# Moving the second group normalization's dependent steps to the end of a stage, with fronts begun four stages later

## The chip, the core and the metric

The kernel runs on one core of a Trainium2 chip. The core has a matrix engine (PE; its weight loads are shown as PEld), a vector engine (DVE, VectorE), a scalar engine (ACT, ScalarE), POOL (GpSimd) and SP (SyncE), which here only issues DMA transfers, as POOL mostly does. Each engine takes its own instructions in the order in which the program gives them, and waits on semaphores for what other engines have to finish. Matrix products land in PSUM, which has eight banks; everything else sits in SBUF or in device memory.

The metric is the time of one execution on the device, in microseconds (us): the median over several runs.

## What is computed

Thirty-two images of 256 channels and 32 x 32 pixels pass through two layers, each after a group normalization over groups of 8 channels, each with a residual addition. The first is a 3x3 convolution on fp16 operands with its result clamped and rounded to fp16. The second is an involution: a small network makes 49 weights for each pixel and each of 16 channel groups, and every output pixel is the sum of its 7x7 neighbours, each times its weight.

```python
x = x + conv3x3_fp16(_gn(x), weight) + bias

z = _gn(x)
y = relu(bn(einsum('oc,bchw->bohw', w1, z)))         # 256 -> 64 channels
w = einsum('oc,bchw->bohw', w2, y) + b2              # 64 -> 16 groups * 49 taps
patches = all 49 shifts of pad(z, 3)
x = x + einsum('bgkhw,bgckhw->bgchw', w, patches)
```

`_gn` takes the mean and the variance over 8 channels and all 1024 pixels and returns (v - mean) / sqrt(var + eps).

## The kernel before

**The loop.** All of the kernel is one loop over steps `n` (line 556, stages in the words of the title), 16 steps to an image (`per`, line 547). What is given in a step is given to all engines in the order of the loop's body; nothing reorders it later. Below, the *phase* of a step is `n` modulo 16, and even and odd phases differ: image `b`'s products `sums` (line 508) come at even steps from n = 16b on, eight times two bands of columns and rows, and write one of two `acc` tiles; `add_windows` (line 530) adds the result into `x` on VectorE one step later, at odd phases. `weights` (line 403) comes at even phases, 18 steps ahead of the sums (`LEAD`): 32 small matmuls into two PSUM banks `pw0`, `pw1`, and four to eight VectorE additions (`evict`, line 424) that put the bias on and move them to the ring `w_sb`.

**From weights to sums.** SP writes the rows of `w_sb` to a buffer `wd` in device memory (`scatter`, line 465), and POOL and SP read it back in another layout into one of three `bands` (`load_bands`, line 478), nine steps ahead of the sums that use it. The image itself is read at line 106 by SP, 63 steps ahead (`LOAD`), and written at line 543.

**The front.** For each image a generator `front(b)` (line 284) gives what comes before the weights, one piece per step, from 56 steps ahead (`FRONT = -56`). So three or four fronts are alive at once, one image apart. Its steps t, counted from its begin, are:

| t | what | engine |
|---|---|---|
| 0, 1 | sums over the image, `add_up` (L214) | ScalarE |
| 2 | first group sum, `mean`, two squares with sums (L214) | VectorE, ScalarE |
| 5 to 7 | second group sum, `s`, `ve`; `r`; `finish` | both |
| 8, 9 | `xq`, the normalized fp16 image (L273) | ScalarE |
| 9 to 26 | convolution in four units of 2 x 9 matmuls (L332), each unit over four steps | PE |
| +3, +4, +5 of a unit | `q` (L346) empties `pc`, `x` (L348) adds bias and residual, `add_up` sums for the second normalization | VectorE, VectorE, ScalarE |
| 27 | first group sum, `mean`, squares of the second normalization | VectorE, ScalarE |
| 29, 30, 32 | second group sum, `s`, `ve`; `r`; `finish` | both |
| 33, 34 | `xn`, the normalized image (L273) | ScalarE |
| 36 | `py` (L377), then `y` (L388) | PE, ScalarE |
| 42, 44, 46, 48 | transposes `pt` (L396), copied to `pixels` (L400) | PE, ScalarE |

A group sum (`group`, line 218) is four VectorE instructions in a chain: `sums` (L222, in the second normalization's first group sum only), `across` (L224), `total` (L226), `back` (L230). `finish` is eight small ScalarE instructions in a chain.

**The order within a step.** In a step every live front is first advanced once, oldest first; this gives its piece. A front that yields `LATER` instead is advanced a second time, behind the first pieces of all fronts and still ahead of `sums`, `add_windows` and `weights`. Both normalizations give their two group sums in that second round.

**PSUM.** The eight banks are given out: `pw0` and `pw1` one each, `acc` two of two banks, `pc` one, and one that `py` and `pt` share. So a convolution unit's first matmul waits until `q` of the unit before has emptied `pc`; a unit's matmuls are at odd phases and `q` at phases 0, 4, 8 and 12.

The loop's advance of the fronts, before:

```python
later = list(fronts)
for part in range(2):
    for b in list(later):
        got = next(fronts[b], fronts)
        ...
        if got is not LATER:
            later.remove(b)
```

Of the kernel before, what the change touches and what calls it, by code (L numbers as in the profile page):

```python
# [69 lines left out]
SCRATCH = 4096  # L70
EARLY = CH + 4 + CH * CR
LATE = K1 * SW + 2 * 2 * SW
FRONT = -56
LOAD = -63
LEAD = 18

# [2 lines left out]
def tile_quant_conv_then_involution(  # L79
# [113 lines left out]
    def quantize_weights(kh):  # L193

        nc.vector.tensor_scalar(wq[:, kh], staged[kh], F16_MAX, -F16_MAX, ALU.min, ALU.max)  # L195
        nc.gpsimd.memset(bands[kh], 0.0)
        if kh == CH - 1:
            nc.gpsimd.memset(w_sb, 0.0)
# [74 lines left out]
                nc.scalar.activation(dst, src, AF.Identity, bias=self.off[:, one], scale=self.rstd[:, one])  # L273

    LATER = 1

    def backwards(at):

        step, n = at.ap[-1]
        return bass.AP(tensor=at.tensor, offset=at.offset + step * (n - 1), ap=[*at.ap[:-1], [-step, n]])  # L280
# [3 lines left out]
    def front(b):  # L284


        xt = x_tiles[b]

        def stages(n):
            for _ in range(n):  # L290
                yield

        gn = GroupNorm(b, 0)
        gn.begin(1)
        for h in range(CH):
            gn.add_up(xt, 0, h, 0, N, AF.Identity)
            yield
        yield LATER
        gn.means()
        gn.squares(xt)  # L300
        yield from stages(3)
        yield LATER
        gn.variances()
        yield
        gn.scales()
        yield
        gn.finish()

        for h in range(CH):
            yield  # L310
            gn.apply(h, [(xq[:, h], xt[:, h].rearrange("p (r c) -> p r c", c=W))])
        gn = GroupNorm(b, 1)
        gn.begin(N // NT)
        units = [(nt, mh) for nt in range(N // NT) for mh in range(CH)]
        for s in range(4 * len(units) + 2):
            u, i = divmod(s, 4)
            if u < len(units):
                nt, mh = units[u]
                if i == 0 and b == 0 and u % 2:

                    pc = ps_m.tile([P, NT], F32, tag="m", name="pc")
                elif i == 0:
                    pc = ps_c.tile([P, NT], F32, tag="pc", name="pc")
                for n in range(sum(CONV[:i]), sum(CONV[: i + 1])):


                    k = n if n < K0 * K0 else CH * K0 * K0 - 1 - n
                    kh, k = n // (K0 * K0), (k + K0 * K0 // 2) % (K0 * K0)
                    di, dj = k // K0 - PAD0, k % K0 - PAD0
                    r0, r1 = max(nt * RT, -di), min((nt + 1) * RT, H - di)  # L330
                    c0, c1 = max(0, -dj), min(W, W - dj)
                    nc.tensor.matmul(  # L332
                        pc.rearrange("p (r c) -> p r c", c=W)[:, r0 - nt * RT : r1 - nt * RT, c0:c1],
                        wq[:, kh, k, mh * P : (mh + 1) * P],
                        xq[:, kh, r0 + di : r1 + di, c0 + dj : c1 + dj],
                        start=n == 0,
                        stop=n == CH * K0 * K0 - 1,
                    )

            u, i = divmod(s - 3, 4)  # L340
            if 0 <= u < len(units) and i < 3:
                nt, mh = units[u]
                cols = slice(nt * NT, (nt + 1) * NT)
                if i == 0:
                    q = work.tile([P, NT], F16, tag="q", name="q", bufs=1)
                    nc.vector.tensor_scalar(q, pc, F16_MAX, -F16_MAX, ALU.min, ALU.max)  # L346
                elif i == 1:
                    nc.vector.scalar_tensor_tensor(  # L348
                        xt[:, mh, cols], q, bias_sb[:, mh : mh + 1], xt[:, mh, cols], ALU.add, ALU.add
                    )  # L350
                else:
                    gn.add_up(xt, nt, mh, nt * NT, (nt + 1) * NT, AF.Identity)
            yield
        yield LATER
        gn.means()
        gn.squares(xt)
        yield from stages(2)
        yield LATER
        gn.variances()
        yield  # L360
        gn.scales()
        yield from stages(2)
        gn.finish()
        xn = work.tile([P, CH, N], F32, tag="xn", name=f"xn_{b}", bufs=1)

        for h in range(CH):
            yield
            to = xn[:, h].rearrange("p (k d r j) -> p d k r j", d=SIDES, r=TR, j=JC)
            at = xt[:, h].rearrange("p (k r d j) -> p d k r j", d=SIDES, r=TR, j=JC)
            gn.apply(h, [(to[:, 0], at[:, 0]), (to[:, 1], backwards(at[:, 1]))])  # L370
        yield from stages(2)

        py = ps_m.tile([P, NT], F32, tag="m", name="py")
        for kh in range(CH):
            px = xn[:, kh].rearrange("p (a i n) -> p a i n", i=2, n=2 * JC)
            for i in range(2):
                nc.tensor.matmul(  # L377
                    py[i * CR : (i + 1) * CR],
                    w1_sb[:, kh, :],
                    px[:, :, i],  # L380
                    start=kh == 0,
                    stop=kh == CH - 1,
                )
        to = y_sb[b % 2].rearrange("p (k r d j) -> p d k r j", k=K, d=SIDES, j=JC)
        of = py.rearrange("p (k d r j) -> p d k r j", k=K, d=SIDES, j=JC)
        for d in range(SIDES):
            at = of[:, d]
            nc.scalar.activation(to[:, d], backwards(at) if d else at, AF.Relu, bias=bn_shift, scale=bn_scale)  # L388
        yield from stages(5)

        for m in range(0, M, 2):
            yield
            pt = ps_m.tile([P, 2, C], F32, tag="m", name="pt")
            for i in range(2):
                for h in range(CH):
                    nc.tensor.transpose(  # L396
                        pt[:, i, h * P : (h + 1) * P], xn[:, h, (m + i) * P : (m + i + 1) * P], ident
                    )
            to = pixels[(b * M + m) // 2 % NPIX].rearrange("p i a (v c) -> p (i a) v c", c=GC)
            nc.scalar.copy(to[:, :, ::2], pt.rearrange("p i (a v c) -> p (i a) v c", v=2, c=GC))  # L400
            yield
# [138 lines left out]
    def store(b, k):  # L540

        cols = slice(k * NT, (k + 1) * NT)
        nc.sync.dma_start(out[b].rearrange("(h p) n -> p h n", p=P)[:, :, cols], x_tiles[b][:, :, cols])
# [5 lines left out]
    def due(n, lag):  # L549

        b, i = divmod(n - lag, per)
        return (b, i) if 0 <= b < B else (None, None)

    with tc.manual_schedule():
        fronts = {}
        for n in range(FRONT, B * per + 2):
            b, i = due(n, FRONT)
            if i == 0:
                fronts[b] = front(b)
            later = list(fronts)  # L560
            for part in range(2):
                for b in list(later):
                    got = next(fronts[b], fronts)
                    if got is fronts:
                        fronts.pop(b)
                    if got is not LATER:
                        later.remove(b)
            if n in (FRONT + CH, FRONT + CH + 4):
                quantize_weights((n - FRONT - CH) // 4)
            b, i = due(n, 0)  # L570
            if b is not None and i % 2 == 0:
                sums(b, i // 2)
            b, i = due(n, 1)
            if b is not None and i % 2 == 0:
                add_windows(b, i // 2)
                if i // 2 == M - 1:
                    store(b, 1)
                    x_tiles.pop(b)

            b, i = due(n, 2)  # L580
            if b is not None and i == 2 * (M - 1 - SIDES):
                store(b, 0)
            b, i = due(n, -LEAD)
            if b is not None and i % 2 == 0:
                weights(b, i // 2 * WR)

            for part in range(2):
                b, i = due(n, -LEAD + 1 + part)
                if b is not None and i % 2 == 0:
                    for k in range(K):  # L590
                        if i // 2 == min((k + 1) * TR // WR, H // WR - 1):
                            scatter(b, k, part)
            b, i = due(n, LOAD)
            if i == 0 and b > 1:
                x_tiles[b] = load_x(b)

            b, i = due(n, 3 - 4 * NBAND)
            if b is not None and i % 4 == 0:
                load_bands(b, i // 4)
# [38 lines left out]
```

## Time and profile before

| | |
|---|---|
| median of 3 runs | 1353.61 us (1353.46 to 1360.37) |
| the profiled execution | 1351.29 us, its span 1349.5 us |
| PE busy | 1247.6 us, 92% of the span |
| POOL busy (issuing DMA) | 1012.5 us, 75% |
| VectorE busy | 827.1 us, 61% |
| ScalarE busy | 734.2 us, 54% |
| DMA | 361.85 MB, 268 GB/s over the span |
| PE waiting for bands, whole span | 44.2 us in 19 waits |

The profile is of one execution. Its page gives the busy time of each engine and of 16 DMA engines together, and the span in 40 slices of 33.7 us, in each of which a digit is the busy share in tenths. Other views list who waited for whom, single instructions in order of time with the wait ahead of each in brackets (length and releaser), and busy times in any stretch that one asks for. A wait "<- issue" is one for which the profile shows no releaser.

The chain of work that ended last gives PE 58% and DMA 24% of the span. The first of image 0's `x<-acc` additions starts at 93.4 us: what lies ahead of it is called the ramp below. The convolutions end three images before the kernel does, and what follows is called the tail.

### The profile page before, as it was taken

What the parts mean: (1) busy time and instruction counts of PE and PEld (TensorE: products, weight loads), DVE (VectorE), ACT (ScalarE), POOL (GpSimd) and SP (SyncE); (2) the same over time, 40 slices, a digit from 0 to 9 for tenths busy, and PEclk for the clock granted to TensorE, in tenths of its full rate; (3) what the DMA queues carried; (4) which work ended last, traced back from release to release, by engine and by line L of the source; (5) the groups of instructions that cost most, each with busy time, mean ns of one, the idle gap of its engine ahead of it and who ended that gap; (6) DMA issues with size and microseconds to landing.
All of it is one profiled execution on the core that took longest, in us unless ns stands there. A gap on an engine that the chain in (4) does not pass through costs nothing.

```text
span 1349.5 us, 65799 instructions
## 1 busy us (share of the span) xinstructions
PE 1247.6 (92%) x27648; PEld 757.6 (56%) x27648; DVE 827.1 (61%) x2539; ACT 734.2 (54%) x1731; POOL 1012.5 (75%) x1818
## 2 busy tenths in 40 slices
PE   4899999999989999999999999999999999999664
PEld 2355556655545665555566556555655556555453
DVE  5456656666656666666666566666666566566542
ACT  5875655555646556565555556555656565563300
POOL 9067777787778778877778777777877877788885
PEclk9999999999999999999999999999999999999997
DMA  6089999999999999999999999999999999999995
GB/s 227 6 236 295 270 271 284 283 278 296 282 271 286 297 287 281 298 282 281 267 285 287 260 282 282 271 284 284 288 285 278 274 280 278 277 285 262 282 270 157
DMA packets 360724, 361.85 MB, mean 268 GB/s; under 512 B 75056, under 2 KB 304752, under 8 KB 359152
## 3 DMA queue, kind: packets, MB, share of 16 engines
q1 hardware_dynamic: 278512, 229.38, 56.5%
q0 software_dynamic: 81920, 128.28, 33.5%
q8 instruction: 220, 3.60, 1.1%
q14 instruction: 72, 0.59, 0.1%
HBM read 176.60 MB, written 180.76 MB: 265 GB/s over the span
## 4 chain that ended last, share of the span: by engine, by line
PE 58%; DMA 24%; POOL 8%; issue 4%; DVE 3%; ACT 2%; SPq 1%; POOLq 0%; DVEq 0%; ACTq 0%
PE pc L332 24%; DMA band<-wd 19%; PE acc L522 18%; PE pw L411 10%; POOL band L497 8%; DMA wd<-w_sb 4%; PE py L377 3%; PE pt L396 3%; ACT junk L214 1%; DVE w_sb L435 1%; SPq L476 1%; DVE wq L195 1%; DVE x L538 1%; DMA band<-in_w 1%; DMA out<-x 0%
## 5 line engine op out<-in xcount | busy, mean ns | idle before, releaser
L497 POOL DMA_DIRECT2D band<-wd x1792 | 980.8, 550 | 320.5 <-DMA band<-wd 189.9
L435 DVE TENSOR_TENSOR w_sb<-pw,late_sb 128x224 f32<-128x224 f32 (+7 forms) x1280 | 331.4, 324 | 423.6 <-PE pw L411 423.4
L332 PE MATMUL pc<-xq,wq 128*128 128x496 f16 (+3 forms) x2304 | 535.1, 378 | 25.0 <-ACT xq L273 20.6
L522 PE MATMUL acc<-band,pixels 64*32 64x190 f32 (+1 forms) x16384 | 423.5, 330 | 55.5 <-DMA band<-wd 44.2
L522 PEld LDWEIGHTS acc<-band,pixels 64*32 64x32 f32 x16384 | 301.6, 107 | 164.7 <-issue 88.9
L332 PEld LDWEIGHTS <-wq 128*128 128x128 f16 x2304 | 206.3, 98 | 322.9 <-issue 106.7
L411 PE MATMUL pw<-late_sb,y 64*32 64x224 f32 (+1 forms) x8192 | 285.0, 330 | 14.1 <-issue 12.7
L538 DVE TENSOR_TENSOR x<-acc,x 128x380 f32<-128x380 f32 (+1 forms) x512 | 262.4, 513 | 35.5 <-PE acc L522 26.6
L411 PEld LDWEIGHTS pw<-late_sb,y 64*32 64x32 f32 x8192 | 183.7, 105 | 38.7 <-issue 22.3
L400 ACT COPY pixels<-pt 128x512 f32<-128x512 f32 x128 | 73.8, 577 | 226.5 <-PE pt L396 226.5
L214 ACT ACTIVATE junk<-x 128x512 f16<-128x512 f32 (+1 forms) x192 | 146.4, 762 | 11.9 <-DVE x L348 9.4
L214 ACT ACTIVATE junk<-x,mean 128x1024 f16<-128x1024 f32 x128 | 147.1, 1149 | 4.3
L245 ACT ACTIVATE s<-back,eps 128x2 f32<-128x2 f32 x64 | 18.9, 296 | 178.8 <-DVE back L230 178.8
L273 ACT ACTIVATE xn<-x,off,rstd 128x512 f32<-128x512 f32 x128 | 96.1, 800 | 0.0
L346 DVE TENSOR_SCALAR q<-pc 128x512 f16<-128x512 f32 x128 | 87.2, 681 | 13.3 <-PE pc L332 13.3
L348 DVE SCALAR_TENSOR_TENSOR x<-q,early_sb,x 128x512 f32<-128x512 f16 x128 | 94.7, 740 | 0.3
L396 PE MATMUL pt<-ident,xn 128*128 128x128 f32 x512 | 77.8, 275 | 1.5 <-ACT pixels L400 1.4
L396 PEld LDWEIGHTS pt<-ident,xn 128*128 128x128 f32 x512 | 63.7, 142 | 27.3 <-issue 2.8
L273 ACT ACTIVATE xq<-x,off,rstd 128x1024 f16<-128x1024 f32 x64 | 75.6, 1227 | 0.0
L235 ACT ACTIVATE mean<-back 128x2 f32<-128x2 f32 x64 | 12.6, 196 | 100.0 <-DVE back L230 100.0
L377 PE MATMUL py<-xn,early_sb 128*64 128x512 f32 x256 | 62.2, 605 | 0.9 <-ACT xn L273 0.9
L388 ACT ACTIVATE y<-py,bn_shift,bn_scale 128x256 f32<-128x256 f32 x64 | 32.5, 557 | 23.3 <-PE py L377 23.0
(40 smaller groups left out, 368.2 us busy)
## 6 DMA issues: line engine op xcount, KB each, us to landing
wd<-w_sb SPq DMA_DIRECT2D x896, 160.0 KB
band<-wd POOLq DMA_DIRECT2D x1664, 70.5 KB
x<-in_x SPq DMA_DIRECT2D x64, 512.0 KB
out<-x SPq DMA_DIRECT2D x64, 512.0 KB
band<-wd POOLq DMA_DIRECT2D x128, 60.5 KB
band<-wd SPq DMA_DIRECT2D x128, 50.5 KB
band<-wd SPq DMA_DIRECT2D x128, 40.5 KB
band<-in_w SPq DMA_DIRECT2D x2, 1152.0 KB
```

Of the source, the lines that this page charges most:

```text
L214: nc.scalar.activation(junk[:, n0:n1], src[:, h, n0:n1], func, bias=bias, accum_out=self.sums[:, i : i + 1])
L273: nc.scalar.activation(dst, src, AF.Identity, bias=self.off[:, one], scale=self.rstd[:, one])
L332: nc.tensor.matmul(pc.rearrange("p (r c) -> p r c", c=W)[:, r0 - nt * RT : r1 - nt * RT, c0:c1], wq[:, kh, k, mh * P : (mh + 1) * P], xq[: ...
L346: nc.vector.tensor_scalar(q, pc, F16_MAX, -F16_MAX, ALU.min, ALU.max)
L348: nc.vector.scalar_tensor_tensor(xt[:, mh, cols], q, bias_sb[:, mh : mh + 1], xt[:, mh, cols], ALU.add, ALU.add)
L377: nc.tensor.matmul(py[i * CR : (i + 1) * CR], w1_sb[:, kh, :], px[:, :, i], start=kh == 0, stop=kh == CH - 1,)
L396: nc.tensor.transpose(pt[:, i, h * P : (h + 1) * P], xn[:, h, (m + i) * P : (m + i + 1) * P], ident)
L411: nc.tensor.matmul(pws[i][t * TW : (t + 1) * TW, : dj.stop - dj.start, r], y_sb[b % 2][half, (r0 // 2 + r) * W : (r0 // 2 + r + 1) * W], w ...
L435: nc.vector.tensor_tensor(to, of[:, :, d0:d1], bias[:, :, d0:d1], ALU.add)
L497: queue.dma_start(to, src)
L522: nc.tensor.matmul(at[t * TW : (t + 1) * TW, h, :, f - top : l - top], px[p, a, v * GC : v * GC + TW], of[:, :, a, f - top : l - top, v], ...
L538: nc.vector.tensor_tensor(x_at, of, x_at, ALU.add)
```

## The change

The group sums of the second normalization, and `py` with `y`, are given in a third round at the end of a step, behind `sums`, `add_windows` and `weights`. The empty steps between them are cut from two to one or from two to none, so that the front from its begin to `py` is four steps shorter, and `FRONT` goes from -56 to -52: `pt` and the weights stay where they are against the sums, and the first normalization and the convolution come four steps later against everything else. The rounds are kept in three lists, and a front is put into the list of the round that it asks for.

```diff
-FRONT = -56
+FRONT = -52
...
     LATER = 1
+    LAST = 2
...
                 else:
                     gn.add_up(xt, nt, mh, nt * NT, (nt + 1) * NT, AF.Identity)
-            yield
-        yield LATER
+            if s < 4 * len(units) + 1:
+                yield
+        yield LAST
         gn.means()
         gn.squares(xt)
-        yield from stages(2)
-        yield LATER
+        yield
+        yield LAST
         gn.variances()
         yield
         gn.scales()
-        yield from stages(2)
+        yield
         gn.finish()
...
-        yield from stages(2)
+        yield
+        yield LAST
 
         py = ps_m.tile([P, NT], F32, tag="m", name="py")
...
-            later = list(fronts)
-            for part in range(2):
-                for b in list(later):
+            parts = {0: list(fronts), LATER: [], LAST: []}
+
+            def go_on(part):
+
+                for b in parts[part]:
                     got = next(fronts[b], fronts)
                     if got is fronts:
                         fronts.pop(b)
-                    if got is not LATER:
-                        later.remove(b)
+                    elif got is not None:
+                        parts[got].append(b)
+
+            go_on(0)
+            go_on(LATER)
...
             if b is not None and i % 2 == 0:
                 weights(b, i // 2 * WR)
+            go_on(LAST)
```

By phase, the front's pieces stand as follows before and after. All that is not in the table keeps its phase, the transposes, the sums, the weights, the scatters and the loads among it.

| piece | phase before | phase after |
|---|---|---|
| first normalization: sums; group sum and squares | 8, 9; 10 (second round) | 12, 13; 14 (second round) |
| its second group sum; `r`; `finish` | 13 (second round); 14; 15 | 1 (second round); 2; 3 |
| `xq` | 0, 1 | 4, 5 |
| `q` of the four units | 4, 8, 12, 0 | 8, 12, 0, 4 |
| second normalization: group sum and squares | 3 (second round) | 6 (last round) |
| its second group sum | 5 (second round) | 7 (last round) |
| `r`; `finish` | 6; 8 | 8; 9 |
| `xn` | 9, 10 | 10, 11 |
| `py`, `y` | 12 (first round) | 12 (last round) |

In phase 8 after the change, VectorE's order is `r` of the older front, then `q` of the younger front's first unit, then that step's evictions of weights.

## The prediction

> **What bounds the kernel now.** I read the page's slices first, then the work image by image, then PE's waits, then single rows around one place of the period.
>
> ```profile
> PE   4899999999989999999999999999999999999664
> ...
> DVE  5456656666656666666666566666666566566542
> ACT  5875655555646556565555556555656565563300
> ...
> DMA  6089999999999999999999999999999999999995
> ```
>
> Two resources are full at once from the third slice to the 37th, PE and the DMA engines; VectorE and ScalarE have four tenths free. So what VectorE does is harmless until PE waits for it. The stretches below are one image each, from one image's first `x<-acc` addition to the next one's (columns: length, then busy time of PE, PEld, DVE, ACT, POOL, granted clock, DMA share, GB/s).
>
> ```profile
> 368.70:412.20 43.50, 38.43 (x866) 23.11 (x864) 25.39 (x80) 22.89 (x54) 33.43 (x62) 1.00 0.95 274
> ...
> 451.00:489.20 38.20, 38.20 (x866) 23.08 (x865) 25.33 (x81) 22.78 (x54) 28.73 (x54) 1.00 0.99 290
> ```
>
> The reader is to see 38.2 us: PE's own work for an image, with no pause in it. Longer images hold that same work and pauses. From the first image's addition at 93.4 us to the thirtieth's at 1246.9 there are 29 images, so (1246.9 - 93.4) / 29 = 39.78 us each, 1.58 above PE's own. PE's waits in that stretch:
>
> ```profile
> PE acc L522 <- DMA band<-wd: 17.8, 13, 2.5
> PE pw L411 <- issue: 10.8, 12, 2.4
> PE acc L522 <- DVE q L346: 1.3, 2, 0.7
> ```
>
> Bands that come late, and pauses with no releaser; nothing worth naming from VectorE. DMA's share of 0.97 of 39.78 is 38.5 us an image, as tight as PE.
>
> **The change, part by part.** No instruction is added or removed, on any engine. The sequences of SP and POOL are the same as before, item for item, so no DMA is issued past another. On PE, VectorE and ScalarE the front's pieces move against the rest of the loop.
>
> *Which wait appears.* Take phase as step modulo 16. The normalization's first group sum and the squares go from phase 3, ahead of everything, to phase 6, behind that step's evictions of weights. The second group sum goes from phase 5 to phase 7: one step behind the squares where it was two. The reciprocal `r` goes from phase 6 to phase 8, where the older front is served first, so on VectorE it now stands directly ahead of `q` of the next image's first convolution unit. Queued behind the group sum that waits for the squares are therefore: rest of the group sum, `r` (waits for ScalarE's `s`), `q`, the evictions of phase 8. And `q` empties the only `pc` bank, which the convolution of phase 9 writes next. That place in the profile before, PE and DVE rows:
>
> ```profile
> 540.20 2.08 PE L332 MATMUL pc<-xq,wq 128*128 128x496 f16 x9
> 540.35 1.28 DVE L435 TENSOR_TENSOR w_sb<-pw,late_sb 128x224 f32<-128x224 f32 x4 [1.10 <-PE pw L411]
> 541.55 1.13 DVE L538 TENSOR_TENSOR x<-acc,x 128x380 f32<-128x380 f32 x2
> 542.60 0.68 DVE L346 TENSOR_SCALAR q<-pc 128x512 f16<-128x512 f32 x1
> 544.92 2.08 PE L332 MATMUL pc<-xq,wq 128*128 128x512 f16 x9
> ```
>
> The convolution of phase 7 starts at 540.20 and that of phase 9 at 544.92; between them lie transposes, sums and weights. `q` is done by 543.3, 1.6 us ahead of need. The moved chain ran undisturbed once, in the ramp, for image 0:
>
> ```profile
> 40.35 0.16 DVE L222 TENSOR_TENSOR sums<-sums 128x2 f32<-128x2 f32 x1 [2.91 <-ACT junk L214]
> ...
> 44.05 0.21 DVE L224 STREAM_TRANSPOSE across<-sums 128x32 f32<-128x32 f32 x1
> ...
> 45.09 0.17 DVE L251 RECIPROCAL r<-s 128x2 f32<-128x2 f32 x1 [0.36 <-ACT s L245]
> ...
> 47.39 0.69 DVE L346 TENSOR_SCALAR q<-pc 128x512 f16<-128x512 f32 x1 [2.14 <-PE pc L332]
> ...
> 48.13 3.97 PE L332 MATMUL pc<-xq,wq 128*128 128x512 f16 x18 [0.78 <-DVE q L346]
> ```
>
> From the first row to `r` is 45.09 - 40.35 = 4.74 us, 0.17 more until `q` can start, and from `q`'s start to the matmul that waits for it 48.13 - 47.39 = 0.74: 5.65 us in all. In the changed kernel the first row follows the evictions of phase 6, at 541.55 on the clock above. The phase-9 convolution then starts at 541.55 + 5.65 = 547.20 instead of 544.92: PE stands 2.28 us, once an image. The two additions of phase 7 (1.13 us) fit into the 2.8 us in which VectorE waits for the squares, so they cost nothing; without that cover they would add their 1.13. The evictions of phase 8 come some 2.3 us late too, but the next weights are due only after a convolution (2.08) and sums (1.6), so nothing waits for them. If the chain is shorter than I think, the nearest small row is PE's 0.78 us wait for `q` above; the largest comparable PE wait in the ramp is 2.70 us for `xq`. I take 2.28, since each term is a measured row of the same operation.
>
> *What the gap does to the clock.* Neighbouring stretches of 3.41 us around four gaps in PE (same columns):
>
> ```profile
> 146.06:149.47 3.41, 1.51 (x46) 1.27 (x52) 1.18 (x3) 2.58 (x10) 3.19 (x6) 1.00 1.09 324
> ...
> 743.40:746.81 3.41, 1.03 (x12) 0.44 (x6) 0.57 (x2) 3.38 (x8) 1.81 (x4) 1.00 1.02 299
> 746.81:750.22 3.41, 3.41 (x24) 1.18 (x29) 2.90 (x9) 3.05 (x8) 3.41 (x7) 0.50 0.92 252
> ...
> 1159.82:1163.23 3.41, 1.20 (x25) 0.57 (x30) 1.82 (x5) 2.79 (x5) 2.66 (x5) 1.00 0.96 290
> 1163.23:1166.65 3.42, 3.42 (x92) 2.65 (x74) 0.00 (x0) 0.00 (x0) 3.42 (x8) 0.50 0.99 284
> ```
>
> Where PE was busy 1.2 us or less of such a stretch, the next ran at half clock; with 1.51 it did not. A half-clock stretch made nine convolution matmuls take 3.44 instead of 2.08 and the sums 1.84 instead of 1.60, so it costs 1.60. A stretch turns when it holds some 2.05 us of idle time (between 1.90 and 2.21). If the stretches lie at random against the gaps, a 2.28 us gap does that with chance (3.41 - 2.28 + 2 x 0.23) / 3.41 = 0.47 (0.37 to 0.55 by the two ends): 0.75 us an image (0.59 to 0.88; 0 if the alignment is kind, 1.60 if it always hits).
>
> [...]
>
> *What the gap pays for.* Of the 1.58 us of pauses an image, some go when PE itself is slower: DMA's 38.5 us of work are then spread over some 41.7, a share of 0.92. How much is shown nowhere: between all (0 left) and nothing (1.58 left). I keep a third, 0.5, since the band waits are of the queueing kind and the pauses without releaser less clearly so.
>
> *Ramp.* Image 0's finish, applications and `y` no longer stand behind the third image's sums. After `r` at 45.09: finish 2.1 us to 47.3, one application 1.5, the next image's sum 0.8, the other application 1.5, the third image's sum 1.2, `y` 1.0: 53.3, and weights follow at once; if the delayed convolution units push `y` to the end, 54.3. Before they start at 57.06, so 2.7 us are gained; image 1's own gap of 2.28 takes most back: -0.4. The best case is four whole steps of the 32.0 us and 18 steps between first weights and first sums (57.06 to 89.08): 4 x 1.78 = 7.1.
>
> *Tail.* One convolution unit, 4.0 us of PE, moves from the ramp into the third-last image, where PE is busy 25.63 of 36.0 us; DMA hides it. I count 0.5, at most 4.0. ScalarE's later `py` and `y`, behind the weights of phase 12, feed the weights of phase 14, a convolution and sums later (3.7 us): covered; uncovered, `y` costs its 1.0 an image.
>
> *Sum.* 38.2 + 2.28 + 0.75 + 0.5 = 41.73 an image, 1.95 over 39.78; times 29 is +56.6, with ramp and tail +56.7. The profiled execution has a span of 1349.5 us and 1.8 around it, 1351.29, which is 2.3 below the median of 1353.61 that I add to: **1410 us**.
>
> **Rivals.**
> (a) *The gap is mostly paid by the waits for bands.* PE and DMA are so near each other that all pauses vanish, and no clock is lost: 38.2 + 2.28 - 39.78 = 0.70, x 29 = +20: 1374, or 1367 with the best ramp. For it: the long images have their DMA pauses at 0.93 to 0.95, so these are hiccups that slack cures. Against it: pauses without releaser are nearly half.
> (b) *Not slower.* The four steps saved in the ramp are all that shows: if `q` can start by 544.92 - 0.74 = 544.18 on the clock above, 2.28 us earlier than I reckon, PE never waits, and 2.7 to 7.1 us are gained: 1347 to 1351. This decides if the squares start before the evictions end, or if PE regularly stands at phase 8 for its band anyway. Against it: VectorE's order puts the group sum behind the evictions, and only 13 band waits occur in 29 images.
> (c) *Nothing is absorbed and the clock falls more often.* 2.28 + 0.88 = 3.16 x 29 = +92: 1445; with every gap costing 1.60, 1466. Against: PE's slowdown must relieve the DMA engines.
>
> **How the numbers follow.** The forecast (1385 to 1440) has 0.62, (a) 0.18, (b) 0.12, (c) 0.08. Half a per cent, 6.8 us, is about what can be told from no change: below 1346.8 counts as faster, over 1360.4 as slower. Faster 0.05 and same 0.09 come from (b) and (a)'s fringe; slower 0.86. The range reaches from (a)'s low end to the forecast's upper end, 1364 to 1440, and leaves out (b) and (c).
>
> **What would show it.** PE's waits should have a new row, `pc` waiting for `q`, some 30 times and 60 to 70 us in all, where it has almost nothing now; VectorE's `across` should wait for ScalarE's squares about 1.7 us an image; images should last 41 to 42 us; DMA share should fall to about 0.92; half-clock stretches should appear in the steady part, a dozen or more; first weights near 54 us. I am wrong if `pc` does not wait for `q`, if images stay under 40 us, or if PE waits more for bands than now.

## The result, and the profile after

The changed kernel takes 1384.28 us (median of 6 runs, 1381.64 to 1394.46) against 1353.53 us for the kernel before: a ratio of 1.0259, with a 95% interval of 1.0224 to 1.0294. It is slower, inside the predicted range of 1364 to 1440 us and 26 us below the predicted 1410.

The profiled execution has a span of 1379.8 us, 30.3 longer. Where the time lies shows in three stretches: up to the first `x<-acc` addition 92.4 us (before 93.4), from there to the thirtieth image's first addition 1184.4 us (before 1153.5), and the tail 103.0 us (before 102.6). All of the loss is in the 29 images of the middle: 40.84 us each instead of 39.78.

PE's waits in that middle part, from the same view as before (columns: total us, times, longest):

```profile
PE pc L333 <- DVE q L347: 43.9, 27, 2.2
PE pw L414 <- issue: 8.1, 9, 1.4
PE acc L525 <- issue: 5.9, 9, 1.1
PE acc L525 <- DMA band<-wd: 5.4, 4, 2.3
PE pc L333 <- issue: 1.3, 2, 1.0
PE acc L525 <- DVE x L541: 1.0, 2, 0.7
PE acc L525 <- DMA wd<-w_sb: 0.2, 1, 0.2
```

The first row is new: 43.9 us that the convolution waits for `q`, once in nearly every image. The other rows make 21.9 us, where all of PE's waits together made 37.0 before: the pauses that were there have shrunk, but not vanished.

The chain of work that ended last, in one image around this wait (start, length, what; three dots stand for the rest of the two group sums, the first square, and rows of "issue" of 0.01 to 0.04 us):

```profile
590.62 2.01 PE pc L333 x9
592.63 0.44 PE pt L399 x4
593.07 1.53 PE acc L525 x53
594.59 0.89 PE pw L414 x14
595.49 1.26 DVE w_sb L438 x4
596.75 0.08 DVE sums L222
...
597.56 0.21 ACT mean L235
...
599.08 1.25 ACT junk L214 x2
...
600.35 0.22 DVE across L224
...
601.06 0.30 ACT s L245
...
601.39 0.07 DVE r L251
...
601.47 0.68 DVE q L347
...
602.20 2.06 PE pc L333 x9
```

Read downwards, it is the order that the prediction gave: PE's weights of phase 6 release the evictions, behind them stands the first group sum, then the mean and the squares on ScalarE, the second group sum, `s`, `r`, and only then `q`, which PE needs. For 6.7 us, from 595.48 to 602.20, the chain is off PE, while PE has only 4.65 us of work left to do, up to 600.13. PE's own rows there:

```profile
595.29 2.08 PE L333 MATMUL pc<-xq,wq 128*128 128x496 f16 x9
597.20 0.60 PE L399 MATMUL pt<-ident,xn 128*128 128x128 f32 x4
597.73 1.65 PE L525 MATMUL acc<-band,pixels 64*32 64x190 f32 x64
599.13 1.00 PE L414 MATMUL pw<-late_sb,y 64*32 64x224 f32 x32
602.20 2.06 PE L333 MATMUL pc<-xq,wq 128*128 128x512 f16 x9 [2.07 <-DVE q L347]
```

PE is done with phase 8 at 600.13 and stands for 2.07 us. Over the whole span the chain that ended last now reads as follows; DMA had 24% of it before, VectorE and ScalarE 3% and 2%:

```profile
PE 66%; DMA 13%; DVE 7%; ACT 7%; POOL 4%; issue 3%; SPq 0%; POOLq 0%; ACTq 0%; DVEq 0%
```

### The profile page after: what moved, and what is told of

Read it like the earlier page. It is cut to its first block, busy times and chain, and to the rows that moved or that the text cites. A ratio compares the mean times of both kernels' runs of the same rounds, so it can differ in the third digit from the quotient of the medians.

```text
span 1379.8 us, 65802 instructions
## 1 busy us (share of the span) xinstructions
PE 1255.8 (91%) x27648; PEld 763.2 (55%) x27648; DVE 824.8 (60%) x2539; ACT 741.7 (54%) x1731; POOL 1014.6 (74%) x1818
## 4 chain that ended last, share of the span: by engine, by line
PE 66%; DMA 13%; DVE 7%; ACT 7%; POOL 4%; issue 3%; SPq 0%; POOLq 0%; ACTq 0%; DVEq 0%
PE pc L333 28%; PE acc L525 20%; PE pw L414 12%; DMA band<-wd 9%; ACT junk L214 5%; PE py L380 4%; POOL band L500 4%; DVE w_sb L438 3%; DMA wd<-w_sb 3%; PE pt L399 3%; DVE q L347 1%; DMA x<-in_x 1%; DVE across L224 1%; DVE back L230 1%; DVE total L226 1%
## 5 line engine op out<-in xcount | busy, mean ns | idle before, releaser
L333 PE MATMUL pc<-xq,wq 128*128 128x496 f16 (+3 forms) x2304 | 542.6, 383 | 69.7 <-DVE q L347 49.0
L333 PEld LDWEIGHTS <-wq 128*128 128x128 f16 x2304 | 210.3, 99 | 384.5 <-issue 175.1
L391 ACT ACTIVATE y<-py,bn_shift,bn_scale 128x256 f32<-128x256 f32 x64 | 32.7, 560 | 136.4 <-PE py L380 136.3
L224 DVE STREAM_TRANSPOSE across<-sums 128x32 f32<-128x32 f32 x128 | 26.7, 209 | 99.8 <-ACT junk L214 98.7
```

What stands on the lines that cost most here:

```text
L333: nc.tensor.matmul(pc.rearrange("p (r c) -> p r c", c=W)[:, r0 - nt * RT : r1 - nt * RT, c0:c1], wq[:, kh, k, mh * P : (mh + 1) * P], xq[: ...
```

## The experiments

Three theories were put against each other. *Q*: `q` stands behind the second group sum, which waits for the squares, and behind `r`. *L*: the last round itself, with `py` and `y` behind the weights, holds up what follows (ScalarE's wait for `py` rose from 23.0 to 136.3 us). *F*: the first normalization and the convolution, four steps later, collide with the copies of `pixels` on ScalarE. All kernels are compared by their ratio to the kernel before, run on the same chip.

### Second group sum behind `q`

```diff
         gn.squares(xt)
         yield
-        yield LAST
+        yield
+        yield LATER
         gn.variances()
         yield
         gn.scales()
-        yield
         gn.finish()
```

> The changed kernel with its second group sum of the second normalization moved from the end of phase 7 to phase 8, behind q and ahead of the evictions; r goes to phase 9, in one step with finish. All else, FRONT, py and y included, stays as changed. Theory Q (q stands behind the group sum that waits for the squares, and behind r): the wait of pc for q, 43.9 us in 27 waits in the changed kernel, goes to under 3 us, images fall from 40.8 to about 39.6 us, and the time is 1345 to 1356, as before the change or a little below. Theory L (the last round itself, py and y behind the weights, holds the chain up): nothing of that is touched, 1380 to 1388. Theory F (convolution and first normalization four steps later meet the copies of pixels on ScalarE): not touched, 1380 to 1388.

Measured: 1342.79 us, a ratio of 0.999 (0.996 to 1.0019) to the kernel before, whose median was 1346.06 in these runs. The wait of `pc` for `q` is gone; these are all of PE's waits in the 29 images, which take 39.50 us each:

```profile
PE acc L525 <- DMA band<-wd: 12.7, 12, 2.0
PE pw L414 <- issue: 7.3, 10, 1.1
PE acc L525 <- issue: 3.7, 6, 1.6
PE acc L525 <- DVE q L347: 3.7, 3, 1.4
PE acc L525 <- DVE x L541: 2.8, 4, 1.1
PE pc L333 <- issue: 2.1, 2, 1.6
```

VectorE's rows at the place (the wait ahead of an instruction in brackets):

```profile
577.78 1.10 DVE L541 TENSOR_TENSOR x<-acc,x 128x380 f32<-128x380 f32 x2
578.80 0.68 DVE L347 TENSOR_SCALAR q<-pc 128x512 f16<-128x512 f32 x1
580.68 0.21 DVE L224 STREAM_TRANSPOSE across<-sums 128x32 f32<-128x32 f32 x1 [1.20 <-ACT junk L214]
...
581.37 1.28 DVE L438 TENSOR_TENSOR w_sb<-pw,late_sb 128x224 f32<-128x224 f32 x4
```

VectorE still waits 1.20 us for the squares, but with `q` ahead of that wait instead of behind it, PE does not notice. Everything else of the change, the shorter front, the last round and the later begin, is still in this kernel. So the order on VectorE, `q` behind the second group sum and `r`, is the whole loss that can be told; L and F are out as its cause.

### Last round alone, without the shortening

FRONT at -56, both group sums and `py` in the last round, all empty steps as before the change:

```diff
-        yield LATER
+        yield LAST
         gn.means()
         gn.squares(xt)
         yield from stages(2)
-        yield LATER
+        yield LAST
         gn.variances()
...
-        yield from stages(2)
+        yield from stages(2)
+        yield LAST
 
         py = ps_m.tile([P, NT], F32, tag="m", name="py")
```

> The kernel before (FRONT -56, all its empty steps) with only the place in the step changed: both group sums of the second normalization and py with y in the last round, behind sums, additions and weights. Theory Q: two steps still lie between the squares and the second group sum, so VectorE does not wait for the squares ahead of a q; pc waits for q under 3 us, time 1349 to 1360. Theory L: the last round costs most of the 30 us, 1372 to 1390. Theory F: the phases are those of before, 1349 to 1360.

Measured: 1349.29 us, ratio 1.0031 (0.9988 to 1.0074), 39.64 us an image, no wait of `pc` for `q`. This is what Q and F had expected; the last round alone costs nothing that can be told.

### `py` and `y` back in the first round

```diff
             gn.apply(h, [(to[:, 0], at[:, 0]), (to[:, 1], backwards(at[:, 1]))])
         yield
-        yield LAST
```

> The changed kernel with py and y alone put back into the first round of phase 12; group sums stay in the last round. Theory Q: pc waits for q as long as in the changed kernel (40 to 46 us), time 1378 to 1390. Theory L: ScalarE's wait for py, 136 us in the changed kernel and 23 before, falls back and takes the loss along, 1350 to 1365. Theory F: 1378 to 1390.

Measured: 1386.61 us, ratio 1.0312 (1.0244 to 1.038). The wait stays, here in its 29 images:

```profile
PE pc L333 <- DVE q L347: 51.1, 28, 2.1
```

L is out here too: ScalarE's longer wait for `py` was idle time that nobody waited for.

### The shortening without the last round

The kernel before with FRONT at -52 and the front shortened; the second group sum follows one step behind the squares in the second round, so behind `q`:

```diff
         gn.means()
         gn.squares(xt)
-        yield from stages(2)
+        yield
         yield LATER
         gn.variances()
         yield
         gn.scales()
-        yield from stages(2)
         gn.finish()
...
-        yield from stages(2)
+        yield
 
         py = ps_m.tile([P, NT], F32, tag="m", name="py")
```

> The kernel before with the front shortened by the same four steps and FRONT at -52, but no last round: the first group sum in the second round of phase 7, the second one in the second round of phase 8, behind that phase's q, r and finish in phase 9, py and y in the first round of phase 12. Theory Q: no q stands behind a group sum that waits; pc waits for q under 3 us, and the ratio to the kernel before is 0.99 to 1.005, so the shortening itself costs nothing and brings next to nothing. Theory F (the four steps by which convolution and first normalization come later): 1.02 to 1.03, as in the changed kernel.

Measured: 1350.96 us, ratio 1.0066 (1.0033 to 1.0099). F is out: its phases are those of the changed kernel. But it missed the expected 0.99 to 1.005 by a little, and the longest of PE's waits in its 29 images says why:

```profile
PE py L376 <- ACT xn L273: 13.6, 21, 0.9
```

VectorE's, SP's and POOL's orders are the same here as in the first experiment; the two kernels differ only in where `py` and `y` stand. In the first round, ahead of the sums, `py` comes before `xn` is done, and PE waits for it 21 times, 13.6 us in all; in the last round it does not, and the ratio is 0.999 instead of 1.0066. The wait is longer than the loss; waits for bands are shorter here, 6.9 us in the 29 images instead of 12.7. So with the shorter front the last round is worth some 0.7% for `py`. The changed kernel with `py` in the first round showed no such wait; that PE was late by then anyway would explain it, but no run shows this by itself.

### `r` behind `q`, the group sum left in place

```diff
         gn.variances()
         yield
+        yield LATER
         gn.scales()
         yield
         gn.finish()
```

> The changed kernel with only r moved behind q in VectorE's order, within phase 8 (second round). q still stands behind the second group sum, but no longer behind r and its wait for ScalarE's s. Theory Q: in the trace of the changed kernel q starts at 601.47 and the group sum's last instruction ends at 601.02, so each gap of PE is shorter by 0.45 us, from 2.1 to about 1.65; 27 waits give 30 to 34 us instead of 43.9; less is then absorbed, and the time falls by 6 to 12 us, to 1372 to 1379. Theories L and F: 1380 to 1388.

Measured: 1358.54 us, ratio 1.0102 (1.0036 to 1.0169), against 1.0259 for the changed kernel: about 1.6%, some 21 us, more than the 6 to 12 expected. The gap did shrink as computed, from 2.1 to 1.58 us where it is undisturbed:

```profile
PE pc L333 <- DVE q L347: 30.2, 24, 1.6
```

That is 13.7 us less. The two other parts of the expectation failed: nothing had to be given back (PE's other waits are 20.1 us, much like the 21.9 of the changed kernel), and the half-clock stretches in the 29 images fell from five to one, worth 4 x 1.6 = 6.4 us by the prediction's own row, and 4.2 by PE's busy time in the 29 images (1118.22 us in the changed kernel, 1114.02 here). Of the stretches that the prediction read, the one with 1.90 us of idle time (PE busy for 1.51 of 3.41) was not followed by half clock; a gap of 1.6 us is shorter than that.

### Longer squares

```diff
         gn.means()
+        extra = work.tile([P, N], F16, tag="junk", name="junk", bufs=1)
+        nc.scalar.activation(extra, xt[:, 0], AF.Square, bias=gn.m[:, :1])
         gn.squares(xt)
```

> The changed kernel with one more pass of squares over half an image on ScalarE, of no use, between the mean and the squares of the second normalization: the squares end some 1.15 us later. Theory Q: the undisturbed gap of PE ahead of phase 9 grows from 2.1 to about 3.25 us, one for one, nearly nothing being left to absorb it (+33 us); and, if idle time in a 3.41 us stretch decides over the clock, as the rows of the kernel before say, a gap of 3.25 turns three of four stretches to half clock, some 20 in the steady part where the changed kernel has 5 (+25 us): ratio 1.06 to 1.075. [...] Theories L and F: ScalarE has the room, 1.025 to 1.035.

Measured: 1449.39 us, ratio 1.0795 (1.0737 to 1.0852), a little over the expected range. PE's wait, and the 29 images as one stretch (length, busy PE, PEld, DVE, ACT, POOL, granted clock, DMA share, GB/s):

```profile
PE pc L333 <- DVE q L347: 85.9, 29, 3.3
```

```profile
98.90:1345.80 1246.90, 1144.06 (x25054) 686.44 (x25044) 739.62 (x2287) 698.27 (x1586) 887.12 (x1623) 0.97 0.90 259
```

The gap grew to 3.3 us, as computed, and the clock granted to PE fell to 0.97 in the mean: 23 half-clock stretches of 3.41 us, where the changed kernel has five. ScalarE is busy 698 of 1247 us, so it is not short of time; what costs is that the added pass stands in the chain.

### Second group sum ahead of the additions

```diff
         gn.squares(xt)
         yield
-        yield LAST
+        yield LATER
         gn.variances()
```

> The changed kernel with the second group sum given in the second round of phase 7, ahead of that phase's two additions instead of behind them; nothing else moves. VectorE then waits for the squares first and does the additions (1.1 us) behind the group sum, ahead of r and q. Theory Q with the cover as the prediction has it: q comes later by the additions less the 0.45 us that r waits for s anyway, so the gap grows from 2.1 to 2.7 to 2.9 us, the ratio to 1.04 to 1.06, with more half-clock stretches (10 to 16). If the additions are not what the wait hides, the ratio stays at 1.02 to 1.03.

Measured: 1408.14 us, ratio 1.0479 (1.0395 to 1.0562), with 14 half-clock stretches:

```profile
PE pc L333 <- DVE q L347: 66.2, 28, 2.7
```

The gap is 2.7 us where it is undisturbed. So the wait for the squares does hide the two additions in the changed kernel, as the prediction said, and without that cover they cost.

### All of them side by side

| kernel | `pc` waits for `q`, us (times) | undisturbed gap, us | half-clock stretches in 29 images | us an image | ratio |
|---|---|---|---|---|---|
| before | 0 | - | 2 | 39.78 | 1 |
| changed | 43.9 (27) | 2.1 | 5 | 40.84 | 1.0259 |
| second group sum behind `q` | 0 | - | 0 | 39.50 | 0.999 |
| last round alone | 0 | - | 3 | 39.64 | 1.0031 |
| shortening alone | 0 | - | 2 | 39.86 | 1.0066 |
| `py` in the first round | 51.1 (28) | 2.1 | 11 | 41.28 | 1.0312 |
| `r` behind `q` | 30.2 (24) | 1.6 | 1 | 40.18 | 1.0102 |
| group sum ahead of additions | 66.2 (28) | 2.7 | 14 | 41.88 | 1.0479 |
| longer squares | 85.9 (29) | 3.3 | 23 | 43.00 | 1.0795 |

The waits and the half-clock stretches are those of the 29 images; the latter are counted in the trace's record of the granted clock. Wherever `pc` waits for `q`, the ratio rises with that wait; where it doesn't, no ratio is over 1.0066. The best version, with the second group sum behind `q`, beats the changed kernel by 2.7% and cannot be told from the kernel before. A second `pc` bank, meant to take the wait away from the other side, was not tried: the kernel has all eight banks in use.

## Why the prediction was right, and where it was off

**The mechanism** is shown: the chain of the changed kernel runs through it link by link, and moving two of its links, the second group sum and `r`, behind `q` takes away all of the loss that can be told. VectorE waits 1.79 to 1.80 us for the squares ahead of the second group sum in every one of the 29 images, where the prediction had about 1.7.

**The gap.** Predicted 2.28 us in each image; undisturbed it is 2.07 in the image above. Most of the 0.2 is that PE's step took 4.84 us there where the row of before had 4.72, and that `q` followed `r` after 0.08 us instead of 0.17. But the mean is 43.9 / 29 = 1.51, and this is the first mis-sized term. Only 13 gaps last 1.99 us or more. The chain itself does not vary: in all 29 images the convolution starts 5.52 to 5.54 us after `sums`. In the 13 images with a full gap PE's own step took 4.77 to 4.91 us. In 14 others it took 5.15 to 6.93, mostly through pauses for a band, for an addition or without a releaser, and in two PE had begun phase 7 late; this time came out of the gap. In one image a wait for a band used the gap up:

```profile
350.75 2.08 PE L333 MATMUL pc<-xq,wq 128*128 128x496 f16 x9
...
355.31 1.60 PE L525 MATMUL acc<-band,pixels 64*32 64x190 f32 x64 [2.04 <-DMA band<-wd]
...
357.66 2.06 PE L333 MATMUL pc<-xq,wq 128*128 128x512 f16 x9
```

The prediction let pauses and gaps trade against each other only through DMA's load, not by falling on the same spot.

**The clock.** Predicted 0.75 us an image from such gaps. All five half-clock stretches of the changed kernel follow one (the two of the kernel before followed a band wait of 2.21 us and a pause of 2.38), and 5 x 1.6 / 29 = 0.28. The chance was sized well for a full gap (five of the 13 long ones turned the clock; by the prediction's formula a 2.07 us gap has 0.40), but there were only 13 full gaps, not 29. The price of 1.60 was also somewhat high: PE's busy time in the 29 images is 1112.77 us with no half-clock stretch (second group sum behind `q`), 1130.05 with 14 (ahead of additions) and 1144.06 with 23 (longer squares), so 1.2 to 1.4 us for each. One of the five, PE's busy time in two neighbouring stretches (columns as above):

```profile
108.63:112.04 3.41, 1.42 (x35) 0.72 (x20) 2.15 (x8) 2.60 (x9) 3.38 (x7) 1.00 0.94 258
112.04:115.45 3.41, 3.41 (x39) 1.37 (x45) 2.08 (x5) 3.31 (x10) 2.97 (x6) 0.51 0.91 270
```

A gap of 1.99 us, all of it inside the first stretch, left PE busy for 1.42 us, and the next stretch ran at half clock; with 1.51 the kernel before kept its clock. The longest gap for `q` in the 29 images of any run is 3.3 us: those of 1.6 us came with one half-clock stretch, those of 2.7 with 14 and those of 3.3 with 23. In each trace the half-clock stretches of the 29 images begin whole multiples of 3.41 us apart. Cut at these points, the nine traces have 54 stretches at full clock in which PE was busy for 1.38 us or less, and all 54 were followed by half clock; of 25 with 1.40 to 1.59 us, five were; of those with more, none.

**Pauses left over.** I kept 0.5 us of 1.58 an image. PE's waits other than for `q` are 21.9 us, or 0.76. Together: 38.2 + 1.51 + 0.28 + 0.76 = 40.75 against 40.84 measured. The prediction's 41.73 was too high by 0.77 for the gap and 0.47 for the clock, and too low by 0.26 here; that these did not all point one way helped the total. DMA's share in this stretch, 0.96 before (the prediction reads 0.97), fell to 0.94 and not to 0.92.

**Ramp and tail.** First weights came at 51.1 us, earlier than the predicted 54.3 (before 57.06). Five of these 6 us were gone by the first additions (92.4 against 93.4): image 1's convolution waited 3.48 us for `q` where I had counted 2.28, another convolution 1.31 for `xq` (0.33 before), and between first weights and first additions PE was busy 1.65 us longer (36.48 against 34.83), with a half-clock stretch at 74.6 us. The small net of -0.4 stands at -1.0. The tail cost 0.4, predicted 0.5.

**The rivals.** The one in which pauses pay for the gap (1374) came closer to the measured 1384 than the forecast did, but partly by luck: in 16 images PE's own delays did come out of the gap, yet pauses of 21.9 us were left of 37.0, and the clock did fall. Not slower failed on VectorE's order, as argued, and of the 2.7 to 7.1 us that it hoped for in the ramp only 1.0 was left at the first additions.

## What to carry to other kernels

In an engine that works in order, look at what stands *behind* an instruction that will wait, not only at the work that it does: here a few small VectorE instructions cost 30 us because the one that frees the convolution's only PSUM bank was queued behind them. When a dependent chain is drawn closer, put each link behind the urgent instruction of its step, and check for every link that the time between it and the next covers the chain's latency. With the same shortening, the order alone decided between 0.999 and 1.026.

## What the runs showed that was not expected

The clock made a small stall worth more than its length: between gaps of 1.6 and 3.3 us the sum of the waits rose by 55.7 us (30.2 to 85.9), and the 29 images by 81.7 us (1246.9 - 1165.2). The difference of 26 us goes with 22 more half-clock stretches, for which PE's busy time rose by 30.0 us (1114.02 to 1144.06, 1.37 for each), and other pauses shorter by 3 us. And a place in the order that looked harmless, `py` ahead of the sums, cost 0.7% once the front was shorter: a wait of 13.6 us in 29 images that none of the other eight profiles has there.
